# A two-layer block on one core: TensorE's background work cut into other pieces, and the first projection in two halves

## The chip, the cores and the metric

The kernel runs on one core of a Trainium2 chip. Its time is the device time of one execution in microseconds (us). The core has TensorE (PE: matmuls, with PEld for its weight loads), VectorE (DVE), ScalarE (ACT), GpSimd (POOL) and SyncE (SP), which here issues all transfers. Each engine works off its own instructions in order.

## The reference, cut to what matters

Sixteen images of 64 x 64 points and 96 channels pass through two layers, each behind a normalization by groups of three channels and each added to its input.

Layer 0 upsamples (64 to 128 points a side, by Fourier transforms, here as matrices), applies a 96 to 384 matrix, a polynomial of degree 2, a 384 to 96 matrix, a low pass and a decimation. Layer 1 is a selective scan in four directions:

```python
xz = jnp.einsum('bhwc,pc->bhwp', x, in_proj_w)      # 96 -> 2 x 192
z = silu(z)
xc = silu(conv_general_dilated(xc, conv_w, ...) + conv_b)   # 3 x 3, by channel
xs = jnp.stack([x0, x1, x0[..., ::-1], x1[..., ::-1]], axis=1)
x_dbl = jnp.einsum('bkdl,kcd->bkcl', xs, x_proj_weight)
delta = jax.nn.softplus(dts + dt_bias[None, :, :, None])
h = jnp.exp(dt[..., None] * As[None]) * h + (dt * ut)[..., None] * bt[:, :, None, :]   # 4096 steps
y = jnp.einsum('bkdn,bkn->bkd', h, ct)
```

The four y are added, normalized over the 192 channels, multiplied with z and projected to 96 channels. There are 4 directions x 192 channels x 16 states to be scanned over 4096 points in each image.

## The kernel before, in words

**Units.** The scan of an image is cut into 8 steps (4 stretches of T = 1024 points forwards, then 4 backwards; each does a pair of directions), a step into 6 blocks of 64 channel rows, a block into 4 units j of 4 states. A unit is two tiles of 128 x 1024 (halves e = 1 and e = 0: 32 channels x 4 states each). There are 192 units in an image and 3072 in all. The loop (L872) does for unit n, in this order on the engines:

- DVE scans half 1 (`recur`, L770 forwards or L772 backwards); every fifth unit ("odd") DVE also multiplies it with ct (L906); the last column is kept (L778); ACT makes the decay of unit n+1, half 1 (`decay`, L755: exp of delta times a constant, into one of two PSUM tiles).
- `slot(0)`: a place for background work.
- POOL multiplies half 1 with ct (L915), but not in odd units, and makes the driving term of unit n+2 (`drive`, L761: dtu times bt, both halves).
- DVE scans half 0; PE reads out unit n-1 (`read_out`, L794: eight matmuls with fold_s, after an L787 where a block of the second pair starts).
- `slot(1)`.
- DVE multiplies half 0 with ct (L924); ACT keeps its last column and makes the decay of unit n+1, half 0.
- Every fourth unit ACT copies the finished y out (L805); `slot(2)`.

A block's dtu and delta tiles are fetched one block ahead, bt and ct tiles some units ahead, all on SP's queue.

**Background.** Other work is written as generators; each `yield` ends a piece. `slot` (L852) steps two of them at each of the three places of a unit: first `project` of the next step, then `front` of the next image, or, when that is through, `finish` of the image before. A `Background` keeps `n`, the weight done, behind `at` x slices / positions: PSLICES = 71 for the 72 places of a step, SLICES = 550 for the 576 places of an image. A piece weighs 1, after `yield HEAVY` 2; after `yield WAIT` the next piece waits for place 2.

- `project` (L633) makes, in two halves of TB = 512 columns, the projection pp (L655), pr (L659), and for each of three channel groups v: s = dtw x pr (L666), six ACT instructions for the parts e, d, m and w of softplus (L674 to L681), their sum by four matmuls with the identity (L686), dtu on DVE (L691), a copy of delta on ACT (L692), and two stores (L695, L696). Its PSUM pool has one buffer. The first step's `project` runs by itself ahead of the loop (L738), and then all bt, ct, dtu and delta tiles of the first block are fetched.
- `front` does layer 0 in four chunks of 25 of 100 upsampled rows: x loads (`fetch_x`, L270, two pieces each of a pool of eleven), 96 small matmuls L324, copies L335, then five groups of widen (L278), h_ps (L365), square hsq (L348), o_ps (L377: 15 matmuls, a yield after six), its copy t (L310), narrow (L294), sd and its store (L303). Then the join (L440, L425), a norm, and layer 1's convolution (L482): nine taps into c_ps and one matmul into z_ps (L494) for each tile of 512 columns, then the Silu (L500, L501, with table loads) and `turn` (a copy to columns L467 and stores). Round i = 0 has 8 tiles of 128 channels; round i = 1 has 4 tiles with two half tiles of 64 channels beside each other, and ends in eight transfers of the columns (L513).
- `finish` does the end of layer 1 in 8 tiles: y_ps by three matmuls L551 and two L561, for 128 and then 64 channels, squares (L558, L576), v_ps (L577, L581), ACT's rsqrt (L586, L587), o_ps (L590), e_ps (L594, L599) and the store.

In the loop c_ps, z_ps and all other PSUM tiles of `front` and `finish` share a pool of two banks. Ahead of the loop `front(0)` has eight banks, and so has `finish(15)` behind it.

Of the kernel before, what the change touches and what calls it, by code (L numbers as in the profile page):

```python
# [54 lines left out]
UPS = 100  # L55
# [16 lines left out]
SLICES = 550  # L72
# [7 lines left out]
def tile_two_blocks(  # L80
# [159 lines left out]
    def front(mi):  # L240
# [71 lines left out]
        o_last = None  # L312
        for p0 in range(0, UPS, PP):

            t1 = b18.tile([HW, PP, C], F32, name="t1", tag="b18")
            xr = fetch_x(0)
            for _ in range(3):
                yield
            for cg in range(3):
                u_ps = [bank([HW, 16, PP], "u_ps") for _ in range(2)]  # L320
                for k in range(16):
                    for a in range(2):
                        on = slice(64 * a, 64 * a + 64)
                        nc.tensor.matmul(  # L324
                            u_ps[a][:, k, :], lhsT=xr[k // 8][on, k % 8, :], rhs=up_s[on, p0:p0 + PP],
                            start=True, stop=True,
                        )
                    if k == 7:
                        yield
                if cg < 2:  # L330
                    xr = fetch_x(cg + 1)
                yield
                for a in range(2):
                    c0 = 48 * a + 16 * cg
                    nc.scalar.copy(t1[:, :, c0:c0 + 16], u_ps[a].rearrange("w c p -> w p c"))  # L335
                    yield
# [4 lines left out]
            for g in range(PP // PG):  # L341
# [8 lines left out]
                for j in range(HB + 1):  # L350
# [10 lines left out]
                    if j == 2 and sd is not None:  # L361
                        stow(sd, row - 2 * PG)
                    if j < HB:
                        h_ps[j] = bank([128, PG * UPS], "h_ps")
                        nc.tensor.matmul(  # L365
                            h_ps[j], lhsT=w1t_s[:, 128 * j:128 * (j + 1)],
                            rhs=xu.rearrange("c p q -> c (p q)"), start=True, stop=True,
                        )
                    elif g < PP // PG - 1:
                        xu_ps = widen(t1, g + 1)  # L370
# [90 lines left out]
        for i, n, tiles, both in ((0, 128, 8, 0), (1, 64, 4, 4)):  # L461
# [14 lines left out]
            for t in range(tiles):  # L476
                c_ps = bank([128, 8, HW], "c_ps")
                for tap in range(9):
# [8 lines left out]
                    if tap == 2 and turned is not None:  # L487
                        turn(*turned)
                    if tap % 3 == 2 and tap < 8:
                        yield HEAVY  # L490
# [13 lines left out]
                yield HEAVY  # L504
# [14 lines left out]
    def finish(mi):  # L519
# [19 lines left out]
        for t in range(8):  # L539
# [7 lines left out]
            for ob, n in ((0, 128), (1, 64)):  # L547
                oc = slice(128 * ob, 128 * ob + n)
                y_ps = bank([n, 8, HW], "yc")
                for i, (w, of) in enumerate(((pmat_s[:, 0, oc], y0), (pd_s[:, 0, oc], u0), (pd_s[:, 1, oc], yu))):  # L550
                    nc.tensor.matmul(  # L551
                        y_ps, lhsT=w, rhs=of.rearrange("c (h w) -> c h w", w=HW), start=(i == 0), stop=False
                    )
                if tail is not None:
# [4 lines left out]
                yield HEAVY  # L559
# [18 lines left out]
            yield HEAVY  # L578
# [5 lines left out]
            yield HEAVY  # L584
# [30 lines left out]
    def scan():  # L615


        with ExitStack() as es:
# [9 lines left out]
            banks.append(es.enter_context(tc.tile_pool(name="b_ps", bufs=2, space=PSUM)))  # L628
            aps = es.enter_context(tc.tile_pool(name="sc_aps", bufs=2, space=PSUM))
            yps = es.enter_context(tc.tile_pool(name="sc_yps", bufs=1, space=PSUM))  # L630
            gps = es.enter_context(tc.tile_pool(name="sc_gps", bufs=1, space=PSUM))

            def project(mi, pair, lc, out):  # L633
# [3 lines left out]
                out["rows"] = rows = dctx.tile([2, 2 * NS, T], F32, name="rows")  # L637
                out["delta"] = [dctx.tile([128, T], F32, name=f"delta_d{v}") for v in range(3)]
                out["dtu"] = [dctx.tile([128, T], F32, name=f"dtu_d{v}") for v in range(3)]
                xs_d = image[mi]["xs"]  # L640
                order = (0, 2, 1)

                def fetch_u(v, t):
                    uv = up_.tile([128, TB], F32, name="u")
# [3 lines left out]
                ahead_u = [fetch_u(v, 0) for v in order]  # L648
                for _ in range(4):
                    yield  # L650
                for t in range(0, T, TB):
                    u, ahead_u = dict(zip(order, ahead_u)), []
                    pp = gps.tile([128, TB], F32, name="pp", tag="g")
# [4 lines left out]
                    pr = pj.tile([128, TB], F32, name="pr")  # L658
# [3 lines left out]
                    for i, v in enumerate(order):  # L662
                        if i == 0:
                            yield
                        s = gps.tile([128, TB], F32, name="s", tag="g")
# [7 lines left out]
                        e, d, m, w = (pj.tile([128, TB], F32, name=k) for k in ("e", "d", "m", "w"))  # L673
# [9 lines left out]
                        s = gps.tile([128, TB], F32, name="s", tag="g")  # L683
# [3 lines left out]
                        for _ in range(3):  # L687
                            yield
                        dtu = pj.tile([128, TB], F32, name="dtu")
                        delta = pj.tile([128, TB], F32, name="delta")  # L690
# [6 lines left out]
                        if t + TB < T and i < 2:  # L697
# [40 lines left out]
            for _ in project(*steps[0], ctxs[0]):  # L738
                pass
            bc = {(what, 0, j): fetch_bc(ctxs[0], 0, j, what) for j in range(NQ) for what in range(2)}  # L740
            dtus = {0: fetch_dtu(ctxs[0], 0)}
            deltas = {(0, e): fetch_delta(ctxs[0], 0, e) for e in (1, 0)}
# [114 lines left out]
            def next_step(st, mi):  # L857

                nonlocal step_gen
                if st < len(steps):  # L860
                    if steps[st][0] > mi:
                        ahead_gen.drain()
                    step_gen = Background(project(*steps[st], ctxs[st]), PSLICES, 3 * per_step)
# [196 lines left out]
```

## Time and profile before

| | |
|---|---|
| median of 3 runs | 21514.79 us (21493.7 to 21515.12) |
| the profiled execution | 21508.85 us, span of its records 21507.1 us |
| busy | DVE 19512.2 (91%), POOL 19511.8 (91%), PE 16918.9 (79%), ACT 13741.5 (64%) |
| mean granted TensorE clock | 0.856 |
| first scan starts, last scan ends | 536.2 us, 21342.0 us |
| one image (192 units), second to fifteenth | 1293 to 1317 us; the last, with no next image behind it, 1232 us |
| L761, mean and count | 4536 ns, 3072 |
| L915 | 2361 ns, 2458 |
| a scan (L770, L772), L924, L755 | 2.29 to 2.35 us, 1223 ns, 1116 ns |

How to read it: a group's line has its busy time, the mean of one in ns, then the idle time of its engine just before its instructions and what ended most of it. In the table of waits a line says who waited for whom: us in total, how often, and the longest in us. In a timeline a line is start, duration, engine, line, operation, and in square brackets the idle time before it and its releaser. Matmuls of fp32 are recorded as two passes each, so that four matmuls L686 are eight records. A table by stretches gives for each engine its busy time in that stretch and the number of records.

### The profile page before, as it was taken

To read this page: it belongs to the slowest core of one execution; us is meant where nothing else is said; L and a number is where in the kernel's file an instruction comes from. 1 tells how busy PE (TensorE), PEld (TensorE's weight loads), DVE (VectorE), ACT (ScalarE), POOL (GpSimd) and SP (SyncE) were. 2 spreads that over 40 slices of the span, in tenths; PEclk is the share of its full clock that TensorE was granted. 3 is DMA by queue.
4 is the path that set the end of the run, shared out by engine and by line. 5 is a ranking of instruction groups with operands and counts; after the bars stand their busy time and mean duration, and the time that the engine had idled before them with its cause. 6 is when DMAs were issued, how large, how long until landed. Compare 5 with 4: busy or idle time off the path is not lost. (4 is left out here: it accounts for less than half of the span.)

```text
span 21507.1 us, 273615 instructions
## 1 busy us (share of the span) xinstructions
PE 16918.9 (79%) x98988; PEld 7271.3 (34%) x98988; DVE 19512.2 (91%) x12983; ACT 13741.5 (64%) x20546; POOL 19511.8 (91%) x5538
## 2 busy tenths in 40 slices
PE   7776877878878788787878778788787888878855
PEld 4423324233332333324333242333423333243221
DVE  0999999999999999999999999999999999999997
ACT  3666666667666666666666666676666666666553
POOL 0999999999999999999999999999999999999996
PEclk8887888888889888898888888888898888888877
DMA  2565565656656566565655656566565665656654
GB/s 74 180 207 184 199 224 187 217 192 204 217 189 227 187 218 203 187 228 183 219 197 200 224 191 215 192 208 215 185 227 187 211 203 192 230 184 217 222 186 140
DMA packets 1855466, 4277.13 MB, mean 199 GB/s; under 512 B 449438, under 2 KB 548670, under 8 KB 1852062
## 3 DMA queue, kind: packets, MB, share of 16 engines
q1 hardware_dynamic: 1854110, 4259.62, 58.8%
q8 instruction: 781, 12.80, 0.2%
q14 instruction: 575, 4.71, 0.1%
HBM read 3380.58 MB, written 878.18 MB: 198 GB/s over the span
## 5 line engine op out<-in xcount | busy, mean ns | idle before, releaser
L761 POOL TENSOR_TENSOR b<-dtu,bt 128x2048 f32<-128x2048 f32 x3072 | 13905.1, 4536 | 594.2 <-DMA dtu<-dtu_d 530.5
L755 ACT ACTIVATE da<-delta,a_s 128x1024 f32<-128x1024 f32 x6144 | 6852.3, 1116 | 2859.4 <-DVE b L924 888.2
L915 POOL TENSOR_TENSOR b<-b,ct 128x1024 f32<-128x1024 f32 x2458 | 5804.1, 2361 | 1235.6 <-DVE new L778 832.6
L794 PE MATMUL y<-b,fold_s 128*32 128x256 f32 x49152 | 3837.1, 435 | 1111.6 <-DVE b L924 551.4
L924 DVE TENSOR_TENSOR b<-da,ct 128x1024 f32<-128x1024 f32 x3072 | 3756.5, 1223 | 93.9
L770 DVE TENSOR_TENSOR_SCAN da<-da,new,b 128x1024 f32<-128x1024 f32 x1383 | 3246.5, 2347 | 282.8 <-ACT da L755 274.7
L772 DVE TENSOR_TENSOR_SCAN da<-da,new,b 128x1024 f32<-128x1024 f32 x1382 | 3242.4, 2346 | 125.5 <-ACT da L755 119.1
L794 PEld LDWEIGHTS y<-b,fold_s 128*32 128x32 f32 x49152 | 1392.0, 119 | 3857.0 <-issue 1333.0
L778 ACT COPY new<-da 128x1 f32<-128x1 f32 x2764 | 434.6, 157 | 2786.4 <-DVE b L924 2294.7
L772 DVE TENSOR_TENSOR_SCAN b<-da,new,b 128x1024 f32<-128x1024 f32 x922 | 2157.9, 2341 | 47.0 <-ACT da L755 46.1
L770 DVE TENSOR_TENSOR_SCAN b<-da,new,b 128x1024 f32<-128x1024 f32 x921 | 2156.6, 2342 | 41.1 <-ACT da L755 39.5
L482 PE MATMUL c_ps<-xgp,wtap_s 96*128 96x512 f32 (+1 forms) x4608 | 1721.3, 642 | 203.6 <-ACT row L500 199.1
L686 PE MATMUL s<-w,ident_s 128*128 128x512 f32 x1536 | 1175.4, 857 | 872.0 <-ACT w L681 752.3
L666 PE MATMUL s<-pr,dtw_s 128*128 128x512 f32 x1536 | 939.0, 696 | 544.6 <-ACT delta L692 328.0
L365 PE MATMUL h_ps<-xu,w1t_s 96*128 96x500 f32 x1920 | 1059.4, 652 | 306.7 <-ACT hsq L348 124.2
L377 PE MATMUL o_ps<-w2c_s,hsq 128*100 128x96 f32 x9600 | 1031.9, 266 | 170.0 <-ACT hsq L348 143.7
L772 DVE TENSOR_TENSOR_SCAN da<-da,b 128x1024 f32<-128x1024 f32 x461 | 1055.9, 2291 | 118.4 <-ACT da L755 116.7
L770 DVE TENSOR_TENSOR_SCAN da<-da,b 128x1024 f32<-128x1024 f32 x460 | 1053.4, 2290 | 106.5 <-ACT da L755 104.3
L377 PEld LDWEIGHTS o_ps<-w2c_s,hsq 128*100 128x100 f32 x9600 | 966.1, 178 | 357.2 <-ACT hsq L348 184.9
L686 PE MATMUL s<-e,ident_s 128*128 128x512 f32 x1536 | 1022.9, 755 | 0.0
L482 PEld LDWEIGHTS c_ps<-xgp,wtap_s 96*128 96x128 f32 (+1 forms) x4608 | 600.1, 172 | 1154.9 <-issue 873.0
L787 PE MATMUL y<-y,ident_s 128*128 128x512 f32 x768 | 534.1, 784 | 538.6 <-ACT yt L805 537.1
(128 smaller groups left out, 21920.7 us busy)
## 6 DMA issues: line engine op xcount, KB each, us to landing
dtu<-dtu_d SPq DMA_DIRECT2D x1536, 512.0 KB
delta<-delta_d SPq DMA_DIRECT2D x1536, 512.0 KB
bt<-rows SPq DMA_DIRECT2D x1024, 512.0 KB
ct<-rows SPq DMA_DIRECT2D x1024, 512.0 KB
u<-xs_d SPq DMA_DIRECT2D x896, 256.0 KB
dtu_d<-dtu SPq DMA_DIRECT2D x768, 256.0 KB
delta_d<-delta SPq DMA_DIRECT2D x768, 256.0 KB
xr<-in_x SPq DMA_DIRECT2D x768, 128.0 KB
```

The source lines that it names most:

```text
L365: nc.tensor.matmul(h_ps[j], lhsT=w1t_s[:, 128 * j:128 * (j + 1)], rhs=xu.rearrange("c p q -> c (p q)"), start=True, stop=True,)
L377: nc.tensor.matmul(o_ps[:, p, :], lhsT=hsq[j][:, UPS * p:UPS * (p + 1)], rhs=w2c_s[:, j, :], start=(j == 0), stop=(j == HB - 1),)
L482: nc.tensor.matmul(c_ps[p:p + n], lhsT=wtap_s[:, tap, 128 * i:128 * i + n], rhs=xgp[:, h0:h0 + 8, dx:dx + HW], start=(tap == 0), stop=(tap ...
L666: nc.tensor.matmul(s, lhsT=dtw_s[:, pair, v, :], rhs=pr, start=True, stop=True)
L686: nc.tensor.matmul(s, lhsT=ident_s, rhs=of, start=(k == 0), stop=(k == 3))
L755: nc.scalar.activation(da, deltas[n // NQ, e], AF.Exp, scale=a_s[:, k, g, units[n][2]:units[n][2] + 1])
L761: nc.gpsimd.tensor_mul(b, dtus[n // NQ], bt.unsqueeze(1).to_broadcast([128, 2, T]))
L770: nc.vector.tensor_tensor_scan(out, da, b, before, ALU.mult, ALU.add)
L772: nc.vector.tensor_tensor_scan(out[:, ::-1], da[:, ::-1], b[:, ::-1], before, ALU.mult, ALU.add)
L794: nc.tensor.matmul(y[32 * q:32 * q + 32, e, :], lhsT=fold_s, rhs=b[:, e, QT * q:QT * q + QT], start=(pair == 0 and j == 0 and e == 0), sto ...
L915: nc.gpsimd.tensor_mul(h, h, bc[1, r, j])
L924: nc.vector.tensor_mul(bs[n][:, 0, :], h, bc[1, r, j])
```

## The change

1. The softplus sum in `project` is cut: after two of its four matmuls there is a yield, and one yield less behind it.
2. The convolution yields with weight 1 after every second tap in place of weight 2 after every third; `turn` comes at tap 3; the piece after the Silu weighs 1. The round of 64 channels comes first.
3. In `finish` the three matmuls L551 are cut after the second, and several yields weigh 1 in place of 2: 14 a tile in place of 16.
4. Layer 0's x loads are asked for further ahead: two at the first chunk's start, and those of the next chunks during the last group of the chunk before; the three yields after a chunk's first load are left out in three of four chunks.
5. SLICES is 499 in place of 550. An image's front then takes weight 368 on 425 places (389 on 408 before), the finish 126 on 146 (142 on 149).
6. The first step's `project` runs as two generators, one for each half, stepped in turn, in a PSUM pool of four buffers; the second half has its own tiles in the buffers b16 and b18. As soon as both halves of the first channel group are stored, the first block's dtu and delta and one bt are fetched; the other bt and ct follow at the end. The loop's PSUM pools are opened after that.

```diff
-SLICES = 550
+SLICES = 499
...
+        asked = []
         for p0 in range(0, UPS, PP):
...
-            xr = fetch_x(0)
-            for _ in range(3):
-                yield
+            if not asked:
+                asked += [fetch_x(0), fetch_x(1)]
+                for _ in range(3):
+                    yield
             for cg in range(3):
+                xr = asked.pop(0)
...
-                if cg < 2:
-                    xr = fetch_x(cg + 1)
+                if cg == 0:
+                    asked.append(fetch_x(2))
...
+                    if j >= 2 and g == PP // PG - 1 and p0 + PP < UPS:
+                        asked.append(fetch_x(j - 2))
...
-        for i, n, tiles, both in ((0, 128, 8, 0), (1, 64, 4, 4)):
+        for i, n, tiles, both in ((1, 64, 4, 4), (0, 128, 8, 0)):
...
-                    if tap == 2 and turned is not None:
+                    if tap == 3 and turned is not None:
                         turn(*turned)
-                    if tap % 3 == 2 and tap < 8:
-                        yield HEAVY
+                    if tap % 2 == 1:
+                        yield
...
                 turned = t, row, z
-                yield HEAVY
+                yield
...
                         y_ps, lhsT=w, rhs=of.rearrange("c (h w) -> c h w", w=HW), start=(i == 0), stop=False
                     )
+                    if i == 1:
+                        yield
...
                     nc.scalar.activation(sq[0], yc[0], AF.Square)
-                yield HEAVY
+                yield
...
             nc.tensor.matmul(v_ps, lhsT=mean_s, rhs=sq[0], start=True, stop=False)
-            yield HEAVY
+            yield
...
                 ahead = fetch_y(t + 1)
-            yield HEAVY
+            yield
...
                             nc.tensor.matmul(s, lhsT=ident_s, rhs=of, start=(k == 0), stop=(k == 3))
-                        for _ in range(3):
+                            if k == 1:
+                                yield
+                        for _ in range(2):
                             yield
...
-            for _ in project(*steps[0], ctxs[0]):
-                pass
-            bc = {(what, 0, j): fetch_bc(ctxs[0], 0, j, what) for j in range(NQ) for what in range(2)}
-            dtus = {0: fetch_dtu(ctxs[0], 0)}
-            deltas = {(0, e): fetch_delta(ctxs[0], 0, e) for e in (1, 0)}
+            with tc.tile_pool(name="side_ps", bufs=4, space=PSUM) as side:
+                todo = [project(*steps[0], ctxs[0], side, 0), project(*steps[0], ctxs[0], side, TB, far.get)]
+                while todo:
+                    todo = [g for g in todo if next(g, todo) is not todo]
+                    if ctxs[0]["made"] >= 2 and not dtus:
+                        bc[0, 0, 0] = fetch_bc(ctxs[0], 0, 0, 0)
+                        dtus[0] = fetch_dtu(ctxs[0], 0)
+                        for e in (1, 0):
+                            deltas[0, e] = fetch_delta(ctxs[0], 0, e)
```

## The prediction

> **What bounds the kernel now.** I read the page's sums first, then the groups, then the waits of the loop, then one image cut into stretches. The page's first part and its dearest groups:
>
> ```profile
> DVE  0999999999999999999999999999999999999997
> POOL 0999999999999999999999999999999999999996
> ...
> L761 POOL TENSOR_TENSOR b<-dtu,bt 128x2048 f32<-128x2048 f32 x3072 | 13905.1, 4536 | 594.2 <-DMA dtu<-dtu_d 530.5
> ...
> L915 POOL TENSOR_TENSOR b<-b,ct 128x1024 f32<-128x1024 f32 x2458 | 5804.1, 2361 | 1235.6 <-DVE new L778 832.6
> ```
>
> GpSimd has two jobs per unit and nothing else: 13905.1 + 5804.1 = 19709 us, 6.42 a unit. The first scan starts at 536.2 and the last ends at 21342.0, so the loop of 3072 units takes 20806 us: 1097 us are GpSimd's idle time, 536 lie ahead of the loop and 165 behind it. More than 6.42 a unit can only come from waits. Who makes DVE wait inside the loop (us in total, times, longest), and who makes ScalarE wait:
>
> ```profile
> DVE da L770 <- ACT da L755: 379.0, 366, 3.4
> DVE da L772 <- ACT da L755: 235.8, 240, 4.0
> DVE dtu L691 <- PE s L686: 235.0, 129, 13.3
> DVE b L772 <- ACT da L755: 177.6, 88, 4.7
> DVE b L770 <- ACT da L755: 72.6, 58, 22.0
> ```
>
> ```profile
> ACT t L310 <- PE o_ps L377: 333.6, 165, 6.3
> ACT hsq L348 <- PE h_ps L365: 300.4, 160, 5.8
> ...
> ACT row L500 <- PE c_ps L482: 107.8, 48, 4.4
> ```
>
> So DVE's waits are 865 us for a decay (L755) that stands late in ScalarE's queue and 235 us for the softplus sum. The decay is late because the background instruction ahead of it waits for TensorE. The timeline shows one such place:
>
> ```profile
> 7349.51 1.05 PE L686 MATMUL s<-w,ident_s 128*128 128x512 f32 x2
> 7349.71 0.56 ACT L310 COPY t<-o_ps 100x480 f32<-100x480 f32 x1 [3.24 <-PE o_ps L377]
> ...
> 7352.11 1.02 PE L686 MATMUL s<-m,ident_s 128*128 128x512 f32 x2
> ...
> 7353.17 0.69 DVE L691 TENSOR_TENSOR dtu<-s,u 128x512 f32<-128x512 f32 x1 [2.72 <-PE s L686]
> ```
>
> TensorE is behind: ScalarE has stood 3.24 us, and DVE stands 2.72 us until the eight passes of the sum (0.43 us apart) are through. One image (the sixth) by stretches; the columns are PE, PEld, DVE, ACT, POOL busy, then the granted clock:
>
> ```profile
> 7108.00:7591.00 483.00, 395.00 (x3093) 215.51 (x3091) 447.26 (x300) 320.62 (x503) 450.76 (x129) 0.86 0.55 187
> ...
> 7732.00:7870.00 138.00, 121.75 (x537) 48.41 (x537) 118.95 (x82) 105.19 (x140) 121.29 (x36) 0.96 0.56 196
> 7870.00:7955.00 85.00, 74.88 (x381) 24.15 (x380) 76.61 (x54) 64.24 (x90) 78.42 (x23) 0.90 0.66 216
> 7955.00:8314.00 359.00, 307.78 (x1354) 102.44 (x1356) 352.63 (x242) 214.29 (x308) 344.71 (x99) 0.92 0.71 231
> ...
> 20600.00:21200.00 600.00, 344.30 (x1810) 117.95 (x1810) 587.80 (x385) 333.23 (x468) 598.42 (x171) 0.72 0.54 189
> ```
>
> GpSimd's idle time is span minus POOL: 32 us in layer 0's chunks, 17 + 7 = 24 (conv, first and second round), 14 in the end of layer 1 and the columns; with some 4 in the norms, 74 an image, times 15 is the 1097. The last line is an image with projections alone in the background: 1.6 us idle in 600. So the projection costs nothing by itself; TensorE must also have another piece.
>
> **The change part by part.** The sum is made against the profiled execution, 21508.85 (span 21507.1); the median of the runs is 5.9 above it.
>
> **Start, on the path.** Before: the last column copy ends at 424.5, eight stores issue for 5.77, the first projection's matmul runs at 433.45, then six links of 11.65 us one after the other (439.7 to 451.3 is one), last delta store at 514.9, then eight row loads stand ahead of dtu and delta on SP, and GpSimd starts at 531.5, its first L915 at 540.4. After: a chunk's first x loads are asked for a group earlier (TensorE's waits at two of three chunk starts, 4.8 and 1.3, and a third like the second: -7); the last column goes out in four stores (2.85 at the first round's end, so -3). The two halves then share three links. One link needs ScalarE 2 x 3.57, three half sums of 1.7 (full clock) to 3.4 (half clock) behind the later chain, and 1.7 for DVE and delta: 14 to 19 us, three of them 42 to 57; pp and pr for both halves some 14, as the second half's u waits for the column buffer. Its first dtu and delta come during the links, so after the last store GpSimd still does one L761 for a bt that lands some 4 us later: first L915 nine us after it, at 486 to 501 in place of 540.4. I take -47; kept -60 to -25.
>
> **Loop, TensorE's pieces.** Counted from the order of TensorE's instructions in both kernels: what is queued from one read-out (L794) to the next, at full-clock durations of this trace (0.86 a 512-column matmul, 0.43 for a pair on half columns, 0.22 for 96 or 100 columns, 0.07 for L324, 1.07 for a read-out). The whole is the same, 893.6 us an image. Of 192 units 44 hold more than 6.4 us before and 39 after; what lies above 6.4 sums to 59.5 and to 50.0. By stage: chunks 15.8 to 10.2, conv 22.4 to 20.7, end of layer 1 18.1 to 15.9. I let the idle time of a stage follow its overload.
> - Chunks: DVE's waits are 79% for decays, so 25 of the 32 us; 35% less is 9 an image, -135. Below: all 25 cannot go, since ScalarE's own bursts stay; I keep -250. Above: 0.
> - Conv: 24 us, 8% less, -28. The last piece before the Silu falls from 3.44 us (three taps and z) to 1.72; L500's 107.8 us is all that can go there, so -110 at best. Against it: a tile of the long round now takes 2.29 units, not 2.43. If a tile's time (18 us: eight tiles on 19.5 units of 7.36, the mean over the 14 images with both neighbours) is set by TensorE, the same time falls on fewer units, 0.14 x 6.42 = 0.9 more idle for each of eight tiles: +105.
> - End of layer 1: 12% of 14 us, -26; but v_ps is read one slot after its matmul, not two. It waits 11.7 us now; at the price of t (334 us on 320, also one slot's lead) 128 of them would cost +133. I take +26, so 0; kept -60 to +130.
> - The x loads of later chunks: L324 waits 62 us for xr in all, on TensorE, off the path: nothing. They take two more buffers of the pool of eleven, and a load on SP that waits for one holds up dtu and delta behind it. SP stands 2765 us behind L691 already, and GpSimd waits for a DMA only some tens of us in the loop: nothing.
>
> **Loop, the sums.** The last two matmuls go one slot later, behind that slot's other piece, while DVE's L691 keeps its slot. A piece in the chunks is (4.83 - 1.07 - 1.29) / 2.86 = 0.85 us (work per unit, less read-out and projection, by pieces per unit). For the 129 waits of today that is 129 x 0.85 = +110; a third less overload takes some 50 of it: +60. Ends: -80 (a third of 235, if only the overload counts) and +310 (half of the 762 in the loop wait 0.85 longer).
>
> Sum: -47 - 135 - 28 + 0 + 60 = -150, so 21508.9 - 150 = 21359, **21360**.
>
> [...] The granted clock is 0.96, 0.90 and 0.92 where TensorE is dense, 0.72 in the image with little to do. My count leaves work per unit nearly as it is (chunks 4.83 to 4.69, long conv round 5.80 to 5.76, end 5.06 to 5.24), so I charge nothing for the clock. [...] At 0.86 in place of 0.96 the first conv stretch would need 121.75 x 0.12 = 14 us more an image, +210, and the sum would be +60.
>
> **The rivals.**
> - Only the start gains. Overload is counted over whole units, and conv backs up more in a denser round; chunks gain and conv and sums give it back. 21508.9 - 47 = 21462; 21440 to 21510.
> - The stalls are thresholds: the decay of half 1 has 2.35 + 1.22 - 1.12 = 2.45 us of slack (scan and multiply of half 0 less its own time), the other 2.35 - 0.16 - 1.12 = 1.07, and many waits of ScalarE are just past it. Then 40% of 1097 goes: 21508.9 - 47 - 440 = 21020; 21000 to 21220. For it: GpSimd's 1.6 idle us in 600 with the projection alone.
> - Slower: DVE waits for the sum. L691 stands between two scans or behind the multiply; a sum a piece later makes DVE, and then L915 and both decays, late. It decides once every second L691 waits 0.85 longer: +310, with the other terms -47 - 135 - 28 + 310 = +100, 21609. For it: 129 waits now, up to 13.3 us. Against it: L691 mostly has a whole unit.
>
> **How the numbers follow.** Forecast (21220 to 21440) 0.55; only the start 0.20; thresholds 0.12; sums late 0.13. The range leaves out the slower case's 0.12 and about half of the thresholds': 21140 to 21550; the forecast's own is 21220 to 21440. About 0.2% (43 us) is what a measurement here can tell from no change: faster 0.55 + 0.12 + half of 0.20 = 0.77, same 0.12, slower 0.11.
>
> **What would show it.** Right: first L915 near 493; GpSimd's idle time in the chunks 20 to 25 us an image, DVE's waits for a decay near 700 in all; L691's wait 250 to 350. Wrong: L691 over 500 (sums), chunks still at 30 (overload was not the cause), conv over 35 (the density), or a first L915 after 515.

## The result

The changed kernel takes 21739.41 us (median of four runs, 21717.09 to 21748.99), the kernel before 21505.53 (four runs): a ratio of 1.0108, 95% interval 1.009 to 1.0125. It is slower by some 234 us, and the forecast of 21360 (21140 to 21550) missed it on the wrong side.

The profile after, of an execution of 21748.99 us (span 21747.2, mean granted clock 0.847). In the code after, L761 is L794, L915 is L948, L755 is L788, L770 and L772 are L803 and L805, L691 is L702, L686 is L696, L482 is L487, L500 is L505, L576 is L583, L581 is L588, and the read-out L794 is now L827. The page's sums and groups:

```profile
DVE  0999999899998989999899998999989899998997
...
POOL 0999999899998989989899998999989999998996
...
L794 POOL TENSOR_TENSOR b<-dtu,bt 128x2048 f32<-128x2048 f32 x3072 | 13895.2, 4532 | 582.0 <-DMA dtu<-dtu_d 468.0
...
L948 POOL TENSOR_TENSOR b<-b,ct 128x1024 f32<-128x1024 f32 x2458 | 5799.3, 2359 | 1492.7 <-DVE new L811 1030.9
```

GpSimd's work is what it was (13895.2 + 5799.3 = 19694.5). The rows of nines now have eight eights each, spread over the whole loop, and the wait for DVE in front of L948 grew from 832.6 to 1030.9. The first scan starts at 495.8 (536.2 before), so the start gains 40 us. The loop from there to the end of the last scan takes 21088 us (20806): it loses 282; the two together are the difference of the two profiles (240), but for 2 us behind the loop.

Who makes DVE wait after, from 470 us on (us in total, times, longest):

```profile
DVE dtu L702 <- PE s L696: 425.6, 179, 14.4
DVE da L805 <- ACT da L788: 401.3, 291, 5.7
DVE da L803 <- ACT da L788: 240.7, 249, 2.0
DVE b L805 <- ACT da L788: 194.0, 121, 4.9
...
DVE b L803 <- ACT da L788: 13.2, 9, 3.3
```

The four waits for a decay are 849 us, as many as before (865, of which 22 stand ahead of the first scan). Of the 425.6 us for the sum 28.7 lie ahead of the first scan; in the loop it is 397 (235 before). What is new stands on TensorE, which waits for ScalarE:

```profile
PE c_ps L487 <- ACT row L505: 343.1, 105, 6.5
...
PE v_ps L588 <- ACT sq L583: 186.4, 67, 6.7
```

Before, these were 199.1 us (82 times) and 71.1 (41 times).

**Where in an image.** I cut images 2 to 15 by the unit in which each stage's first piece comes, and took from each stage 6.416 us per unit, GpSimd's work (19709 / 3072). What is left is waiting, in us per image, a mean over the 14 images:

| | chunks | conv | end of layer 1 | the rest | all |
|---|---|---|---|---|---|
| before | 27.5 | 25.6 | 10.6 | 9.9 | 73.6 |
| after | 17.5 | 36.7 | 22.6 | 14.6 | 91.3 |
| difference x 14 | -140 | +155 | +168 | +66 | +249 |

The first and the last image add 33: 249 + 33 = 282. GpSimd's idle time ahead of its own instructions in the same units says much the same: chunks 37 to 28, conv 28 to 40, end 14 to 26. So the gain forecast for the chunks came, and the conv and the end of layer 1 each took more than it.

### The profile page after: what moved, and what is told of

It reads as the page before. It is cut to its first block, busy times and chain, and to the rows that moved or that the text cites. A ratio compares the mean times of both kernels' runs of the same rounds, so it can differ in the third digit from the quotient of the medians.

```text
span 21747.2 us, 273372 instructions
## 1 busy us (share of the span) xinstructions
PE 17146.1 (79%) x98988; PEld 7239.8 (33%) x98988; DVE 19544.9 (90%) x12983; ACT 13775.6 (63%) x20546; POOL 19508.4 (90%) x5538
## 5 line engine op out<-in xcount | busy, mean ns | idle before, releaser
L794 POOL TENSOR_TENSOR b<-dtu,bt 128x2048 f32<-128x2048 f32 x3072 | 13895.2, 4532 | 582.0 <-DMA dtu<-dtu_d 468.0
L788 ACT ACTIVATE da<-delta,a_s 128x1024 f32<-128x1024 f32 x6144 | 6849.1, 1117 | 2993.9 <-DVE b L957 964.0
L948 POOL TENSOR_TENSOR b<-b,ct 128x1024 f32<-128x1024 f32 x2458 | 5799.3, 2359 | 1492.7 <-DVE new L811 1030.9
L827 PE MATMUL y<-b,fold_s 128*32 128x256 f32 x49152 | 3941.0, 445 | 1137.9 <-DVE b L957 692.0
L805 DVE TENSOR_TENSOR_SCAN da<-da,new,b 128x1024 f32<-128x1024 f32 x1382 | 3243.0, 2347 | 291.3 <-ACT da L788 284.9
L803 DVE TENSOR_TENSOR_SCAN da<-da,new,b 128x1024 f32<-128x1024 f32 x1383 | 3246.1, 2347 | 168.6 <-ACT da L788 161.6
L827 PEld LDWEIGHTS y<-b,fold_s 128*32 128x32 f32 x49152 | 1413.3, 121 | 3995.2 <-issue 1534.2
L805 DVE TENSOR_TENSOR_SCAN b<-da,new,b 128x1024 f32<-128x1024 f32 x922 | 2158.4, 2341 | 157.6 <-ACT da L788 156.7
L803 DVE TENSOR_TENSOR_SCAN b<-da,new,b 128x1024 f32<-128x1024 f32 x921 | 2156.3, 2341 | 0.7 <-POOL b L794 0.6
L487 PE MATMUL c_ps<-xgp,wtap_s 96*64 96x512 f32 (+1 forms) x4608 | 1767.2, 642 | 348.5 <-ACT row L505 343.1
L696 PE MATMUL s<-w,ident_s 128*128 128x512 f32 x1530 | 1172.6, 858 | 693.0 <-ACT w L691 599.3
L805 DVE TENSOR_TENSOR_SCAN da<-da,b 128x1024 f32<-128x1024 f32 x461 | 1055.9, 2290 | 124.2 <-ACT da L788 116.4
L803 DVE TENSOR_TENSOR_SCAN da<-da,b 128x1024 f32<-128x1024 f32 x460 | 1053.3, 2290 | 81.3 <-ACT da L788 79.1
L702 DVE TENSOR_TENSOR dtu<-s,u 128x512 f32<-128x512 f32 x765 | 522.2, 683 | 575.3 <-PE s L696 568.4
L487 PEld LDWEIGHTS c_ps<-xgp,wtap_s 96*64 96x64 f32 (+1 forms) x4608 | 595.1, 171 | 1318.6 <-issue 857.0
L696 PE MATMUL s<-e,ident_s 128*128 128x512 f32 x1530 | 1021.0, 757 | 0.0
```

The source lines that it names most:

```text
L487: nc.tensor.matmul(c_ps[p:p + n], lhsT=wtap_s[:, tap, 128 * i:128 * i + n], rhs=xgp[:, h0:h0 + 8, dx:dx + HW], start=(tap == 0), stop=(tap ...
L696: nc.tensor.matmul(s, lhsT=ident_s, rhs=of, start=(k == 0), stop=(k == 3))
L788: nc.scalar.activation(da, deltas[n // NQ, e], AF.Exp, scale=a_s[:, k, g, units[n][2]:units[n][2] + 1])
L794: nc.gpsimd.tensor_mul(b, dtus[n // NQ], bt.unsqueeze(1).to_broadcast([128, 2, T]))
L803: nc.vector.tensor_tensor_scan(out, da, b, before, ALU.mult, ALU.add)
L805: nc.vector.tensor_tensor_scan(out[:, ::-1], da[:, ::-1], b[:, ::-1], before, ALU.mult, ALU.add)
```

## The experiments

The theory first formed from this: TensorE meets a piece that waits for ScalarE one place sooner than before (two yields around v_ps and the one behind the Silu weigh 1 in place of 2), stands there, and all that is queued behind it is late. The first rival: the finer cuts (denser conv, sum a place later) are at fault. The second: each part gains, and the parts spoil each other. Every kernel below is the kernel before (L numbers differ by a few) with the edit shown or named; the paces are set so that a stage ends at the place that is wanted. Layer 0's front and the finish then have numbers of their own:

```diff
-SLICES = 550
+SLICES = 527
+LATE = 550
...
-                    behind_gen = Background(finish(mi - 1), SLICES, POS)
+                    behind_gen = Background(finish(mi - 1), LATE, POS)
```

"532/550" below means front 532, finish 550. The medians with the kernel before on the same chip, and the waiting per image as in the table above:

| kernel | us | ratio, 95% | first scan | chunks | conv | end | rest |
|---|---|---|---|---|---|---|---|
| a1_start | 21460.6 | 0.9978 [0.9969, 0.9988] | 497.4 | 27.4 | 25.0 | 10.9 | 9.2 |
| a2_sum | 21449.5 | 0.9977 [0.9968, 0.9986] | 535.6 | 25.6 | 22.0 | 11.0 | 11.3 |
| a3_taps, 532/550 | 21635.7 | 1.0063 [1.0048, 1.0078] | 545.9 | 16.9 | 37.8 | 13.0 | 13.2 |
| a4_finish, 550/487 | 21618.2 | 1.0054 [1.0037, 1.007] | 539.0 | 26.4 | 25.6 | 20.0 | 9.3 |
| b1_fetch, 536/550 | 21455.8 | 0.998 [0.9971, 0.999] | 532.5 | 25.2 | 20.7 | 13.0 | 11.2 |
| b2_pace, 527/550 | 21370.3 | 0.9943 [0.9926, 0.9959] | 536.3 | 16.6 | 21.0 | 15.2 | 11.4 |
| b3_order | 21421.1 | 0.9965 [0.9952, 0.9978] | 541.3 | 27.1 | 19.4 | 11.3 | 9.9 |
| c1_taps_heavy | 21428.7 | 0.9969 [0.9957, 0.998] | 543.4 | 26.7 | 21.6 | 10.5 | 9.3 |
| c2_coarse_light, 532/550 | 21772.5 | 1.0126 [1.0111, 1.0141] | 543.9 | 16.9 | 46.8 | 12.6 | 12.7 |
| d1_v_light, 550/487 | 21649.9 | 1.0069 [1.0054, 1.0084] | 538.8 | 26.9 | 25.5 | 21.6 | 9.6 |
| c4_without, 515/550 | 21647.9 | 1.0068 [1.0051, 1.0084] | 493.6 | 21.9 | 30.8 | 16.9 | 15.3 |
| e1_uncut, 515/550 | 21563.1 | 1.0029 [1.0018, 1.004] | 488.0 | 20.9 | 28.4 | 15.6 | 14.0 |
| e2_pace_cut, 527/550 | 21407.8 | 0.9958 [0.9943, 0.9973] | 545.4 | 18.1 | 21.9 | 16.2 | 11.1 |
| e3_start_pace_taps, 527/550 | 21360.1 | 0.9937 [0.992, 0.9954] | 494.5 | 17.1 | 22.1 | 14.0 | 11.3 |
| e4_pace535, 535/550 | 21437.0 | 0.9971 [0.996, 0.9982] | 545.5 | 14.8 | 27.4 | 15.3 | 11.2 |
| f1_start_pace, 527/550 | 21344.6 | 0.9923 [0.9906, 0.9939] | 499.6 | 16.9 | 21.0 | 14.9 | 11.4 |
| f2_order_pace, 527/550 | 21473.1 | 0.9986 [0.9977, 0.9995] | 499.5 | 17.7 | 28.7 | 17.0 | 11.2 |
| f3_heavy_again, 515/550 | 21666.5 | 1.007 [1.0055, 1.0085] | 496.9 | 21.5 | 33.3 | 16.5 | 14.9 |

The kernel before measured 21498.7 to 21508.05 beside them; differences below are to its median on the same chip. The stages are read from one profiled execution each, which lay up to 21 us from the median (e1's 20 below, f2's 21 above).

### One part alone

**a1_start** has part 6 only (the diff of the first `project`, as shown above).

> The kernel before with only the start of the change: first projection as two generators in a pool of four PSUM buffers, early fetches; pieces, weights and SLICES as before. Every theory: the first scan near 496 in place of 536 us, the loop unchanged at 20800, so 21465 (0.998). If the loop feels the other order of PSUM pools or tiles, it is off by more than 20 us from that.

-44 us, with the loop as before (20799 against 20806 us). The start's term holds, and it stands apart from everything else.

**a2_sum** has part 1 only:

```diff
+                            if k == 1:
+                                yield
-                        for _ in range(3):
+                        for _ in range(2):
```

> The kernel before with only the softplus sum cut into two pieces. Theory 'pieces' (a later last half keeps DVE waiting): DVE's wait for the sum rises from 235 to some 400 us, time +100 to +200 (1.005 to 1.009). Theory 'pace' (only the density of the background costs): within 20 us of before, DVE's wait below 280.

DVE waits 396 us for the sum in place of 235, as 'pieces' had it, and the kernel is still 55 us faster, by the conv (25.6 to 22.0), which neither theory had. That wait is no measure of the loss.

**a3_taps** has the convolution's cuts and weights of part 2, without the exchange of the rounds:

```diff
-                    if tap == 2 and turned is not None:
+                    if tap == 3 and turned is not None:
...
-                    if tap % 3 == 2 and tap < 8:
-                        yield HEAVY
+                    if tap % 2 == 1:
+                        yield
...
                 turned = t, row, z
-                yield HEAVY
+                yield
```

> The kernel before with only the taps in pieces of two at weight 1 (round order as before); the front's slices are 532, so that its 377 of weight take the 408 places that 389 took, the end's 550 stay. Theory 'pieces': conv is 8 to 12 us an image slower, +100 to +180. Theory 'pace': at the old extent the smaller pieces are neutral or better, -30 to +20.

+131 us. The chunks gain 10.6 us an image and the conv loses 12.2. The first piece of the next tile now comes in the very next place behind the Silu in all 12 tiles of an image; before, that was so in 7 of 12 and two places later in 5. TensorE waits for a c_ps bank 105 times, 244 us (199 before). A second thing changes with the weight: the twelve tiles weigh 72 in place of 84 and take 78 places in place of 88 (26 units, 29.3 before), so the convolution is also denser.

**a4_finish** has part 3 only (the cut behind L551 and the weights).

> The kernel before with only the cuts and weights of the end of layer 1; its own slices are 487, so that 126 of weight take the 149 places that 142 took. Theory 'pieces' (one slot of lead for v_ps and for ScalarE's rsqrt is too little): TensorE's wait for sq rises from 71 towards 190 us, the stage loses 8 to 13 us an image, +120 to +200. Theory 'pace': -30 to +30.

+113 us, all in the end of layer 1 (10.6 to 20.0): TensorE's wait for ScalarE's square in front of v_ps goes from 71 to 215 us.

**b1_fetch** has part 4 only.

> The kernel before with only the earlier x loads and the nine yields fewer; front slices 536, so that its 380 of weight take the 408 places as before. Theory 'cuts of conv and end cost, the rest gains': -20 to -60, in the chunks. Theory 'SP's queue': a load that waits for a buffer holds up dtu and delta, +20 to +100, and GpSimd's or ScalarE's waits for a DMA rise over 100 us.

-43 us, but not where it was expected: the chunks gain 2.3 only, the conv 4.9.

**b2_pace** changes no piece, only the pace: 527/550 as in the diff above, so that the chunks' pieces fall on 74 units in place of 71.

> The kernel before with only the front's slices at 527 in place of 550: 389 of weight on 425 places, as in the changed kernel; the end keeps 550. If the stages' stalls follow the density of TensorE's work, all of the front is 4% less dense: -20 to -60. If it is the place at which pieces happen to fall, anything within +-60, and single stages move by over 5 us an image in both directions.

-129 us, twice what either theory allowed. The chunks lose 10.9 us an image of waiting: all that the changed kernel gains there, without any of its cuts. The end of layer 1, whose pieces are untouched but now fall seven units later, goes from 10.6 to 15.2.

**b3_order** has the exchanged rounds only:

```diff
-        for i, n, tiles, both in ((0, 128, 8, 0), (1, 64, 4, 4)):
+        for i, n, tiles, both in ((1, 64, 4, 4), (0, 128, 8, 0)):
```

> The kernel before with only the round of 64 channels first. All theories: -3 at the start and no more than +-20 in the loop. If more, where the two rounds fall against the projections' sums is what counts.

-78 us, in the conv (25.6 to 19.4), where no theory had more than 20. So five of seven parts gain alone, and the two that lose are the two with weights of 1 next to a wait for ScalarE.

### The weight or the cut

**c1_taps_heavy** is a3_taps with weight 2 kept behind the Silu, at the old pace; **c2_coarse_light** keeps the three taps and changes that one weight, at 532/550; its diff:

```diff
                 turned = t, row, z
-                yield HEAVY
+                yield
```

> The kernel before with the taps in pieces of two at weight 1, but the piece behind the Silu keeps weight 2, so that a tile weighs 7 as before and conv keeps its 38 units (SLICES 550). Theory 'finer cuts cost': conv stays near the 38 us an image of the taps-only run, +100 or more. Theory 'the early piece behind the Silu and the density cost': conv is at 20 to 27, within +-40 of before.

> The kernel before with its pieces of three taps, only the piece behind the Silu weighs 1 in place of 2 (a tile 6, as in the taps-only run; front slices 532, same extent of the front). Theory 'finer cuts cost': conv stays near 26, chunks gain 10 as they do at this pace, -100 to -150. Theory 'early piece and density': conv at 35 to 45 us an image, +50 to +200.

The finer taps with the old weight gain 70 us; the coarse ones with the new weight lose 274, conv 46.8, though the pace of 532 that goes with it takes the chunks down to 16.9. So, in the kernel before, the cut is good and the weight is bad. In c2 the next tile's first three taps come one place behind the Silu, and TensorE's and ScalarE's waits are:

```profile
ACT e L675 <- PE s L667: 320.4, 91, 7.1
...
PE c_ps L483 <- ACT row L501: 262.7, 105, 5.2
```

(before: 89.2 and 199.1). The two banks hold c_ps and z_ps of a tile until the Silu has read them, so the next taps wait on TensorE. Of ScalarE's 320 us for the projection's s, 276 fall on three places of each image (units 106, 119 and 130). One of them:

```profile
7861.26 4.54 PE L483 MATMUL c_ps<-xgp,wtap_s 96*128 96x512 f32 x6 [1.93 <-ACT row L501]
...
7877.38 1.12 PE L667 MATMUL s<-pr,dtw_s 128*128 128x512 f32 x2
...
7878.54 0.60 ACT L675 ACTIVATE e<-s 128x512 f32<-128x512 f32 x1 [6.63 <-PE s L667]
```

TensorE stands 1.93 us for the bank, then works without a gap for 16.12 us until the matmul of s, and ScalarE stands 6.63 us for it, with the next Silu and a decay behind it. At all 45 such places the last wait for a bank, of 1.2 to 3.0 us, lies 15 to 19 us back, and TensorE has not paused for over 0.5 us since. So two things meet: TensorE has stood for a bank, and it is then too full to make that up. The earlier piece brings the one, the denser convolution the other, and a3 and c2 have both; no run takes them apart. c1 has neither more than the kernel before: with weight 2 its tile weighs 7 again and takes the old units.

How a late s reaches GpSimd is seen in the changed kernel (start, duration, engine, line; in brackets the idle time before it):

```profile
8007.59 0.60 ACT L684 ACTIVATE e<-s 128x512 f32<-128x512 f32 x1 [2.13 <-PE s L676]
...
8008.87 1.28 ACT L505 ACT_TABLE_LOAD   x1
...
8010.16 0.69 ACT L505 ACTIVATE row<-c_ps,convb_s 128x512 f32<-128x512 f32 x1
...
8010.90 1.99 PE L487 MATMUL c_ps<-xgp,wtap_s 96*128 96x512 f32 x4 [1.63 <-ACT row L505]
8011.35 1.28 ACT L507 ACT_TABLE_LOAD   x1
8012.65 1.12 ACT L788 ACTIVATE da<-delta,a_s 128x1024 f32<-128x1024 f32 x1
8012.81 1.07 PE L827 MATMUL y<-b,fold_s 128*32 128x256 f32 x16
...
8013.87 2.35 DVE L805 TENSOR_TENSOR_SCAN b<-da,new,b 128x1024 f32<-128x1024 f32 x1 [3.78 <-ACT da L788]
...
8016.55 2.35 POOL L948 TENSOR_TENSOR b<-b,ct 128x1024 f32<-128x1024 f32 x1 [3.02 <-DVE new L811]
```

ScalarE first stands 2.13 us for s. The Silu then holds it 3.76 us (8008.87 to 8012.63), two table loads of 1.28 included, and the decay queued behind starts at 8012.65. DVE stands 3.78 us for it and GpSimd 3.02. TensorE stands 1.63 us for the bank, with the read-out behind it.

**d1_v_light** changes only the two yields around v_ps, at 550/487:

```diff
             nc.tensor.matmul(v_ps, lhsT=mean_s, rhs=sq[0], start=True, stop=False)
-            yield HEAVY
+            yield
...
                 ahead = fetch_y(t + 1)
-            yield HEAVY
+            yield
```

> The kernel before with only the two yields around v_ps at weight 1 in place of 2; L551 and L561 as before; the end's slices 487 (same extent). Theory 'lead' (TensorE waits for the square, all pieces behind it are late): TensorE's wait of v_ps for sq over 150 us in place of 71, the end of layer 1 at 17 to 21 us an image, +80 to +140. Theory 'cut of L551': within +-30.

+151 us, the end of layer 1 at 21.6: these two weights give all that a4_finish loses, and the cut of L551 gives nothing of it. One of its 128 tiles:

```profile
4145.15 0.71 ACT L679 ACTIVATE w<-e,one_s 128x512 f32<-128x512 f32 x1
4145.76 0.58 ACT L577 ACTIVATE sq<-yc 64x512 f32<-64x512 f32 x1
...
4146.39 2.02 PE L582 MATMUL v_ps<-sq,mean_s 64*96 64x512 f32 x2 [2.78 <-ACT sq L577]
...
4149.47 0.67 ACT L587 ACTIVATE sq<-v_ps,eps_n 96x512 f32<-96x512 f32 x1
...
4150.77 2.35 POOL L916 TENSOR_TENSOR b<-b,ct 128x1024 f32<-128x1024 f32 x1 [1.39 <-issue]
```

The square L577 stands in ScalarE's queue behind four instructions of the softplus and a decay. TensorE meets v_ps before it is there and stands 2.78 us. Its two passes then take 2.02 us, where two passes of the same line take 1.10 elsewhere (they took 1.10 at 4301.49). The granted clock is 1.00 before the wait and 0.50 behind it, where TensorE is busy for the whole 7.60 us. The three stretches are before, in and behind the wait; the clock is the third number from the end:

```profile
4139.00:4143.60 4.60, 4.60 (x38) 1.46 (x36) 3.57 (x4) 2.29 (x4) 4.60 (x2) 1.00 0.91 313
4143.60:4146.40 2.80, 0.02 (x3) 0.01 (x1) 1.37 (x2) 2.80 (x6) 2.80 (x2) 0.98 0.99 284
4146.40:4154.00 7.60, 7.60 (x8) 2.00 (x9) 7.53 (x6) 4.68 (x7) 6.21 (x3) 0.50 0.85 305
```

### Parts together

**c4_without** is the changed kernel without the two losing parts: start, cut sum, x loads and order, at 515/550 (the changed kernel's places). **e1_uncut** is that with the sum whole.

> The changed kernel without its taps and without its end of layer 1: start, cut sums, earlier x loads, round order, and the slower pace of the front (380 of weight on 425 places: slices 515; the end 550). If the parts add up as measured alone (-44, -55, -44, -129, -78): -350, 21155. If their gains overlap (pace and x loads both thin out the chunks, order and pace both the conv): -200 to -280.

> As c4_without, but the sum uncut: start, x loads, round order, pace. Theory 'the cut costs at this pace': DVE's wait for the sum falls from 398 to under 200 us, -150 to -250 against before (21250 to 21350). Theory 'places of the conv rounds': conv stays at 30 us an image and the time within +-50 of before's 21500 or over.

Alone, the start, the cut sum, the x loads, the order and a slower pace gave -44, -55, -43, -78 and -129: -349. Together they give +149, and +57 with the sum whole. The second rival is right too: the parts spoil each other, more than any expectation had it. The cut of the sum costs 85 us here (92, each against the kernel before beside it), with DVE's wait for it 398 us against 222.

**e2_pace_cut** is b2_pace with the cut sum; **e4_pace535** is b2_pace with 535 for 527; **e3_start_pace_taps** is b2_pace with the start and c1's taps (weight 2 behind the Silu).

> The kernel before with only the front's slices at 527 and the cut sum. If the two gains add up: -180 (21320). Theory 'the cut costs at this pace': DVE's wait for the sum 350 to 450 us, time 21430 to 21520, that is 60 to 150 over the pace alone (21370).

> The kernel before with only the front's slices at 535, between 550 and 527: 389 of weight on 419 places. If density rules: about 60% of the way, -75 (21425), +-25. If the places rule: off that by 50 us or more.

> The kernel before with the start, the front's slices at 527, and the taps in pieces of two with weight 2 behind the Silu; sum, end of layer 1, round order and x loads as before. If these gains add up: -44 - 129 - 70 = -243 (21255). If the places rule: anywhere from 21250 to 21450.

The cut sum costs 37 us at this pace (21407.8 against 21370.3, beside which the kernel before stood at 21506.0 and 21499.1), where it gained 55 at the old one; DVE's wait for the sum is 279 us, so the time and the wait both lie between what the two theories had. 535 gives -69, which is the -75 of the expectation by density, but its stages do not lie between: the chunks are at 14.8, lower than at 527 (16.6), and the conv at 27.4, higher than at either pace. And the taps that gained 70 alone add nothing to start and pace: -146, where -44 - 129 - 70 = -243 would be the sum.

**f1_start_pace** has start and 527/550; **f2_order_pace** that and the exchanged rounds; **f3_heavy_again** is the changed kernel with its three weights of 1 (behind the Silu, around v_ps) set back to 2, at 515/550.

> The kernel before with the start of the change and layer 0 at the slower pace (SLICES 527, finish 550), nothing else. If the two gains add (-44 and -129 measured alone): 21505 - 173 = 21332, chunks 17 us of GpSimd's idle time an image. If gains of separate parts do not add even for parts that meet nowhere in the loop: 21360 to 21400, as in the kernel that also has the finer taps (21360).

> The same with the 64-channel round of the convolution first. It tells which part spoils the convolution in the kernel with start, order, x loads and pace 515 (28 us an image, 21563). If it is the order at a slower pace: convolution 27 us or more an image, TensorE's wait for ScalarE's row over 300 us, 21400 to 21480. If it is the x loads or the pace of 515: convolution near 20, 21250 to 21330, the best kernel of this study.

> The changed kernel with weight 2 again behind the Silu of the convolution and at the two yields around v_ps, the paces set to leave both stages at the changed kernel's places (515, 550). If these weights are what the change loses by: end of layer 1 from 22.6 to 13 to 16 us an image (-100 to -145), convolution from 36.7 to at most 31 (-85 or more), total 21480 to 21560; what is then left above the kernel before is the meeting of the other parts (21563 and 21648 without the taps and cuts of the end, sum whole and cut). If the weights matter only alone and the order, x loads and sum set the loss: 21620 to 21740, TensorE's wait for ScalarE's square back at 70 us all the same.

f1 is the fastest kernel of this study, 21344.6 (-163, of -173 if the two gains add): parts that meet nowhere do add. With the rounds exchanged, which alone gained 78, it loses 128 of that. Every stage lies on the same units in both, and the conv's 7.7 us come from its last seven units, 135 to 141: they hold 9 us of waiting in f2 and none in f1. In f1 the last matmuls of the convolution come ahead of them (L483 ends near 7907 of the sixth image's 7954), and only the transfers of the columns are left; in f2 these lie behind the first round, and the long round's tiles run on to the end (7994 of 8011). There, in unit 137, TensorE waits for a bank up to 10.3 us at once, 129.5 us of the 251.0 in all (the expectation had over 300):

```profile
PE c_ps L483 <- ACT row L501: 251.0, 58, 10.3
```

(f1: 193.2 us, 63 times, 7.4 at most). Since e1's conv (28.4) is that of f2 (28.7), the order at the later place explains e1's conv; the x loads and the pace of 515 are worth another 90 us by the medians (21563.1 against 21473.1; the two profiled executions are 50 apart), in the chunks (+3.2 us an image) and the rest (+2.8).

f3 lies in the range of the second expectation, though the wait in front of v_ps is not back at 70 us but gone (17.8, from 186). The end of layer 1 falls from 22.6 to 16.5 only (10.6 before) and the conv from 36.7 to 33.3, 9.5 x 14 = 133 us together. TensorE's wait for a bank does not fall at all (350.2 us, 129 times, from 343.1), and e1, with the coarse taps and weight 2, has 329.1: in the changed kernel that wait does not come from the weight behind the Silu. And the chunks give 4.0 x 14 = 56 back, as heavier pieces behind them make their own pace denser (units 7 to 80 in place of 8 to 83). The whole gain is 73 us.

So there is one way down from the best kernel to the changed one: f1 21345, exchanged rounds 21473 (+128), x loads and 515 21563 (+90), cut sum 21648 (+85), finer taps and cut of L551 21666 (+19, less than the 42 us between f3's own runs), weights of 1 and 499 21739 (+73). The sizes belong to this order of steps: the same edits on the kernel before gave -78, -43, -55, -70 (the taps), and +131 to +274 and +151 (the weights).

## Why the prediction was wrong, point by point

- **Start (-47): right.** -44 alone, -40 in the changed kernel. The first L948 came at 504.2, not at 493: the first L794 ran at 468.31, but the second stood 26.92 us for a bt, the stores of whose rows were issued by 444 us but whose fetch is issued at 494.05, behind the last delta store.
- **Chunks (-135): the size right, the cause half right.** -140 was measured. "I let the idle time of a stage follow its overload" held here, but what thinned the overload is the slower pace (b2_pace: 27.5 to 16.6), not the cut of the sum (25.6) or the x loads (25.2).
- **Conv (-28, bounds -110 to +105): wrong, +155.** The step that failed took the waiting from a count of TensorE's work between two read-outs: the count fell by 8% (22.4 to 20.7) while the waiting rose from 25.6 to 36.7 us an image. The count had no term for TensorE standing still, and the sum gave the exchange of the rounds no price at all. The exchange is the larger part that the runs show: it gains 78 at the old pace and costs 128 at the slower one (conv 21.0 in f1, 28.7 in f2). "The last piece before the Silu" was watched, not the first one behind it, whose weight of 1 the diff names: with the denser convolution that comes with it, it costs 131 to 274 in the kernel before, but in the changed kernel setting it back takes away 3.4 of the 11.1 us (f3). The density for which +105 was kept is neither shown nor ruled out: a3 and c2 have it together with the earlier piece, c1 has neither more than the kernel before.
- **End of layer 1 (0, bounds -60 to +130): the mechanism seen, the size not.** "v_ps is read one slot after its matmul, not two" was priced at +26 of its +133. The two weights cost 151 alone. In the changed kernel they are about half of the +168: in f3, with both back at 2, 16.5 us an image stay, and b2_pace, which leaves the finish alone, has 15.2; that the slower front moves the end onto other units had no term. The wait to look at was less that of ScalarE for v_ps (11.7 us before, 52 to 55 in d1 and a4, 10.1 in the changed kernel) than the one ahead of it, TensorE's for the square (71 us before, 186 to 215 with weights of 1): the first of the two yields lies between the square and the matmul that reads it.
- **The rest (+66): no term.** The stretch between the chunks and the conv, and what lies behind the end, stood in the sum at nothing; e1 has 14.0 us an image there, f2 11.2, so more than half of it comes with the x loads and the pace of 515.
- **The sums (+60, wait 250 to 350): the wait right in kind (397 us in the loop), the price unsettled.** DVE's wait rose by 161 us in a2, 146 in e2 and 176 in c4. The time changed by -55, +37 and +85. A wait of DVE in the loop is not time lost until GpSimd waits for it.
- **"I charge nothing for the clock": the clock did change, but the waiting does not follow it.** As a mean over the 14 images TensorE was at half clock for 46 us of the units of an image's conv before and 66 after, and for 44 and 59 of those of its end of layer 1. But a3 loses 12.2 us an image in the conv with 47 us at half clock, and b2 gains 4.6 with 58. (The two conv rows of the prediction's table are cut some 13 us late: the round of 128 channels ran from 7717 to 7858 at 0.95, that of 64 from 7870 to 7942 at 0.94, not 0.96 and 0.90.) The prediction's 0.86 in place of 0.96, with its +210 us, was an estimate. In the changed kernel the sixth image's rounds ran at 0.86 (64 channels, 7812 to 7911) and 0.89 (128 channels, 7911 to 8090), but no run shows what that alone costs. In d1 the clock went to 0.50 behind a gap of 2.78 us, and that gap came from a wait for ScalarE. No run separates the loss by the slower clock from that by the wait ahead of it.
- **The rivals.** "Only the start gains" had the right mechanism in part (the conv and the end give the chunks' gain back) and stopped too early. The slower rival named the sums; that was not it in the kernel before, and is 85 us of it on top of the other parts. That a term's sign would turn with the other parts was in no rival: I added seven terms as if they were independent, and the terms of the loop are not.
- **Of the signs set out:** L702's wait (397 in the loop) stayed under 500 and the waits for a decay at 849, so the mark for sums did not show; conv over 35 did (36.7), and that mark was put down to density, which no run singles out. The waits for a decay did not fall to 700 though the chunks improved: the other stages took them up.

What stays open: whether the weight behind the Silu costs by the earlier piece or by the denser convolution; why the exchange of the rounds is good at one pace and bad at another beyond where its last tiles fall, and why the x loads turn from -43 to a part of +90. The runs show the stretch of units, not which piece of the projection meets which tile there. A kernel that fixes the pieces' places by hand was not tried.

## What to carry to other kernels

Where TensorE works in order, look at each piece that reads what another engine makes, and ask how many places lie between the two: taking one away cost 150 us here for two weights (d1), though TensorE's work was the same, since all that is queued behind it is late too. Pieces that share their places with another stream do not have prices of their own: five edits worth -349 us one by one came to +149 together, so build up from the best version and measure after each step. The plainest edits were the best: a slower pace and a start that overlaps, 21344.6 us, ratio 0.9923 [0.9906, 0.9939].

## What the runs showed of the hardware

The granted clock has two values in the records of the traces before and after, 1.00 and 0.50. What I had not expected is how short a wait can stand ahead of a stretch at 0.50, and how long the stretch is: behind the 2.78 us without a matmul shown in d1's timeline the clock was 0.50 for some 10 us (0.50 from 4146.4 to 4154, 0.69 as a mean from there to 4158), with TensorE busy all the while. In the trace before 734 stretches are at 0.50: 196 of them last 3.41 us, 295 last 6.83, 85 last 10.24, and the others are longer, but for one that the end of the trace cuts off. Over longer stretches of that trace the mean clock is lower where TensorE has less to do: 0.95 where its records fill 127.76 of 144 us (7718 to 7862), 0.72 where they fill 33.17 of 61 (7657 to 7718) and 344.30 of 600 (20600 to 21200). What sets the clock no run singles out.
